# First products of sixteen full expert tiles computed during the state space model, and tiles over the usual number in conditional blocks

## Chip, core and metric

The kernel runs on one core of one Trainium2 chip. The metric is the device time of one execution in microseconds, as the median of several runs; a profiled execution gives the span and the trace that the text reads. The engines are called by their short names: PE is the matmul engine (PEld its weight loads), DVE the vector engine, ACT the activation engine, POOL the general one that also issues indirect transfers, SP the one that here only issues transfers. Everything is in 32-bit floats.

## What is computed

The input has 2 images of 256 channels and 48 × 48 points. A first layer (local attention of 7 × 7 plus a dynamic convolution) is followed by a second layer on the 4608 points as tokens of 256 values: a state space model and then a mixture of eight experts. Only the last is changed in substance:

```python
def _L1_ffn_ref(x, Wg, bg, W1, b1, W2, b2):
    xf = x.reshape(-1, D)
    gate_logits = xf @ Wg + bg
    top_w, top_i = jax.lax.top_k(gate_logits, TOP_K)          # TOP_K = 2
    top_w = jax.nn.softmax(top_w, axis=-1)
    w_dense = jnp.sum(jax.nn.one_hot(top_i, E, dtype=xf.dtype) * top_w[..., None], axis=1)
    out = jnp.zeros_like(xf)
    for e in range(E):                                        # E = 8
        h = jax.nn.gelu(xf @ W1[e] + b1[e], approximate=False)
        out = out + w_dense[:, e:e + 1] * (h @ W2[e] + b2[e])
    return out.reshape(B, L, D)

t = _to_tokens(x)
t = t + _L1_attn_ref(_ln_t(t), ...)                           # the state space model
t = t + _L1_ffn_ref(_ln_t(t), ...)                            # the experts
```

W1 is 256 × 1024 and W2 is 1024 × 256 for each expert. Each token goes to two experts, so there are 9216 rows of work, and how many fall on each expert is known only while the kernel runs.

## The kernel before

**Stages.** `run` issues three stages one after the other: `layer0` (the first layer), `mamba` (the state space model with the routing of the tokens), and `experts`. The memory of a stage (its pools) is given back at its end and used again by the next one.

**The state space model.** The 4608 tokens are 36 chunks of 128, in 12 blocks of three chunks. For a block, `norms`, `project_block` and `decays_of` make the normalized input, its projection, a convolution of four taps and the decays; for a chunk, `chunk` carries the state on and makes the output product (the matmul `out`, line 1419), after which the router's scores of the chunk are known. The chunks are routed in seven groups of 6, 6, 6, 6, 6, 4 and 2 (`GROUPS`). For a group, `gate` takes the top two experts of each token, counts how many rows each expert has so far (`g9`, kept in the tile `before`), and works out for every row its place in the table `xs` in HBM, which has a part of 4864 rows for each expert. The steps `put` (line 1628) scatter the rows of 265 values there (256 of the token, 8 expert weights, 1 token number) by indirect transfers of POOL, two for a chunk.

**What sets the order.** In this stage the order on PE, DVE, ACT and SP is written out ahead by a planner, the class `Flow`. Each step is added by `op` or `chain` with its engine, an estimated cost in ns, the steps that it needs, buffers that it takes and gives back (`room` says how many of each there are), and a due time: the number of its chunk times `PACE1`. The planner goes through a simulated time and starts, on each free engine, the step that is ready with the lowest rank; the rank is the due time less the length of the chain behind the step and less a figure of the step's kind from the table `LEAD1`. The result is the program order of the engines, and each engine executes its own queue strictly in this order. A transfer that SP issues has to wait for whatever produces its data, with everything behind it in SP's queue waiting too.

**The experts.** `experts` works on tiles of one expert's rows: a pair tile has 256 rows, a single tile 128. Since the counts are known only on the chip, the program has a fixed list: 36 pair tiles (`NPAIR`) and 8 single tiles (`NSINGLE`), one single after every four pairs. That is enough for any routing. `plan`, a chain of small DVE operations, makes from the counts two lists of where each tile's rows begin and which expert it has; what is over points to rows of zeros. `fill` writes 256 such rows behind the last row of each expert. For each tile, SP loads two numbers into registers (`value`) and issues the transfers with them (`fetch`: rows `ex`, weights `wt` of 2184 KB); `turn` transposes the rows on PE and copies them to `ext` by DVE, and takes the row weights; `up` is the first product, eight column blocks of two matmuls each, with bias and Gelu on ACT; `down` is the second product, 8 matmuls for each 128 rows into `po`, then bias and row weight on DVE, and an indirect transfer of POOL that adds the rows to `acc` in HBM. The loop is `up(i)`, `turn(i+1)`, `down(i)`, `fetch(i+3)`; there are three buffers of weights and four of rows. The very first tile always belongs to the first expert, and its weights (`first_weights`) are loaded during the state space model. At the end the sums in `acc` are loaded in twelve blocks by SP and ACT, transposed and written out.

Of the kernel before, what the change touches and what calls it, by code (L numbers as in the profile page):

```python
# [37 lines left out]
P = 128  # L38
# [38 lines left out]
NPAIR, NSINGLE = 2 * B * N // TR, E  # L77
NROWS = E * PART + TR
XW = C + E + 1
WCOL = NH * HID + NHC * C + NHC + C + E  # L80
# [143 lines left out]
class Kernel:  # L224
# [685 lines left out]
    def mamba(self, ctx):  # L910
# [8 lines left out]
                    mt=4, yi=1, y=4, sq=2, state=3, rd=2, u2=2)  # L919
# [12 lines left out]
        for g, n in enumerate(GROUPS):  # L932
            self.gate(g, first, n)
            first += n
        self.run_flow()

    PACE1 = 16387
    LEAD1 = {
        "al": -98773, "btt": 13567, "ct": -7065, "cum": 4429, "cv": 6696, "decayed": -3519, "dg":
        43691, "er": -366, "ex": -2395, "from": 164, "g10": 12483, "g5": -503, "g6": 8421, "g8":  # L940
        12831, "g9": 4638, "ge": -8611, "gm": 23689, "gmrs": 24439, "grs": -21221, "gsm": -10849,
        "gsw": 4862, "kap": 26098, "keep": -114, "lg": -10468, "mm": 2057, "mo": -5497, "mrr":
        10080, "mrs": -16433, "msw": -973, "mt": 8168, "n2": 1756, "n4": 12308, "nt": 100439,
        "number": 4867, "out": 3070, "pg": -32761, "place": 5798, "ps": -21172, "pst": 9783, "put":
        -196893, "py": 1458, "rd": -2334, "rg": -181, "row": 17176, "rs": -443, "rs1": 1733, "s0":
        443, "s4": 4537, "silu": -11890, "silub": 4711, "silux": -6634, "sm": -2191, "sq": -5514,
        "ss": -43075, "st": 864, "state": 16912, "stats": -2514, "su": -1714, "tap": 24701, "tb":
        2251, "tc": 62673, "tx": 5481, "u2": -20378, "xc": 12597, "xd": -222, "xo": -4221, "xt":
        45375, "xw": -105, "ya": 3557, "yb": 4919, "yi": -8286, "yz": 759, "z": -8801,
# [539 lines left out]
    def gate(self, g, first, n):  # L1489
# [135 lines left out]
        for i, c in enumerate(chunks):  # L1625
            for q in range(2):
                def put(i=i, q=q):
# [4 lines left out]
                    self.tc.declare_no_dep(ins.ins, group="rows", reason="every row of the table is written once")  # L1632
                    self.tc.add_to_no_dep_group("rows", ins.ins)
# [3 lines left out]

    def plan(self, pool):

# [8 lines left out]
        rows = new("rows", 2, E)  # L1648
        nc.vector.tensor_sub(rows[:, 0, :], self.taken, self.c["base"])
# [68 lines left out]
    def experts(self, ctx):  # L1718
# [12 lines left out]
        for i in range(NPAIR):  # L1731
            tiles.append((2, i))
            if i % every == every - 1 and i // every < NSINGLE:
                tiles.append((1, i // every))
# [238 lines left out]
```

## Time and profile before

| what | value |
|---|---|
| median of 3 runs | 1443.69 us (1443.32 to 1445.69) |
| span of the profiled execution | 1442.1 us (this run: 1443.9 us) |
| mean granted PE clock | 0.965 |
| PE busy in the span | 1312.6 us, 91% |
| DVE, ACT, POOL busy | 824.9, 757.6, 537.7 us |
| moved by DMA | 209.40 MB, mean 145 GB/s |
| last matmul of the state space model's output (line 1419) ends | 794.0 us |
| last scatter of rows lands | 822 us |
| first matmul of an expert tile, last one | 832.1 us, ends 1404.7 us |

Busy time is the time in which at least one instruction of an engine is under way. In the table of stretches that the prediction shows, a row is a stretch of the span in us, its length, then for PE, PEld, DVE, ACT and POOL the busy us and the number of instructions, then the granted clock, the busy share of the DMA engines, and GB/s. In the chain of waits a row is the start and length in us, the engine, what was written, the line and how many instructions were merged. A matmul of 32-bit floats leaves two records in this trace, so 16 matmuls appear as x32.

### The profile page before, as it was taken

How to read it: one execution, taken by the hardware profiler on the slowest of the kernel's cores; microseconds unless marked ns; L12 is line 12 of the kernel's file. 1: busy time of each engine (PE TensorE's matmuls, PEld its weight loads, DVE VectorE, ACT ScalarE, POOL GpSimd, SP SyncE). 2: the span in 40 equal slices, each digit the busy share in tenths (PEclk: the TensorE clock that was granted, in tenths of full speed). 3: DMA queues.
4: the chain of work that ended last, by engine and by line, in shares of the span. 5: the costliest groups of instructions: out<-in, count | busy, mean ns of one | idle time of the engine just before them, and what ended most of it. 6: DMA issues, size and time to landing. Idle time of an engine off the chain costs nothing.

```text
span 1442.1 us, 21771 instructions
## 1 busy us (share of the span) xinstructions
PE 1312.6 (91%) x7480; PEld 1028.6 (71%) x7480; DVE 824.9 (57%) x2165; ACT 757.6 (53%) x1840; POOL 537.7 (37%) x652
## 2 busy tenths in 40 slices
PE   5999999998999898988987099999999999999993
PEld 4566766666666665766665088888888888888883
DVE  5989999997799898999896321111111111111113
ACT  2688787897877767778765022222222222223220
POOL 5213030201666868776877511222212222222220
PEclk9999999998999999999999599999999999999996
DMA  8321412111432333323331276666667666676628
GB/s 289 99 84 44 146 36 94 45 54 67 129 91 81 117 91 101 104 78 118 100 112 52 98 280 216 224 215 196 222 209 225 201 225 205 202 227 215 225 27 266
DMA packets 102157, 209.40 MB, mean 145 GB/s; under 512 B 10251, under 2 KB 87260, under 8 KB 96092
## 3 DMA queue, kind: packets, MB, share of 16 engines
q1 hardware_dynamic: 81692, 181.06, 37.1%
q0 software_dynamic: 14976, 20.26, 7.4%
q10 hardware_dynamic: 5380, 6.69, 1.3%
q8 instruction: 60, 0.98, 0.3%
q14 instruction: 49, 0.40, 0.1%
HBM read 168.20 MB, written 44.71 MB: 148 GB/s over the span
## 4 chain that ended last, share of the span: by engine, by line
PE 53%; DVE 12%; POOL 5%; DMA 3%; issue 2%; ACT 2%; DVEq 0%; ACTq 0%; POOLq 0%; SPq 0%
PE bank L1787 19%; PE po L1801 19%; PE bank L908 3%; PE zbank L908 3%; POOL xs L1628 2%; PE bank L1419 2%; PE bank L894 2%; PE bank L1358 1%; PE bank L1401 1%; DVE xc L1105 1%; DMA out<-o 1%; DVE bc L1105 1%; DVE mt L1321 1%; DMA cz<-bc 1%; DVE yi L1378 1%
## 5 line engine op out<-in xcount | busy, mean ns | idle before, releaser
L1791 ACT ACTIVATE hid<-bank,wt 128x256 f32<-128x256 f32 (+1 forms) x352 | 160.1, 455 | 402.7 <-PE bank L1787 398.6
L1807 POOL DMA_INDIRECT acc<-ey,ex x80 | 124.6, 1557 | 462.6 <-DVE ey L1805 308.9
L1787 PE MATMUL bank<-ext,wt 128*128 128x256 f32 (+1 forms) x1408 | 286.2, 362 | 0.8 <-DVE ext L896 0.8
L1801 PE MATMUL po<-wt,hid 128*128 128x256 f32 x1280 | 283.7, 379 | 0.0
L1787 PEld LDWEIGHTS bank<-ext,wt 128*128 128x128 f32 x1408 | 249.8, 191 | 31.9 <-DVE ext L896 1.2
L1801 PEld LDWEIGHTS po<-wt,hid 128*128 128x128 f32 x1280 | 239.8, 190 | 30.8
L896 DVE COPY ext<-bank 128x512 f32<-128x512 f32 (+1 forms) x44 | 28.3, 643 | 231.4 <-PE bank L894 231.4
L1804 DVE TENSOR_TENSOR ey<-po,wt 128x256 f32<-128x256 f32 x80 | 34.0, 424 | 140.9 <-PE po L1801 140.8
L584 DVE SCALAR_TENSOR_TENSOR x<-hid,w2r,x 128x1128 f32<-128x1128 f32 (+3 forms) x72 | 99.9, 1393 | 0.4 <-ACT hid L578 0.2
L908 PE MATMUL bank<-xn,win 128*128 128x387 f32 x240 | 93.8, 514 | 0.4 <-DVE lg L1444 0.2
L673 POOL COPY kp<-kp 128x10 f32<-128x10 f32 (+1 forms) x60 | 23.6, 394 | 189.0 <-DVE kp L666 189.0
L1313 ACT ACTIVATE mt<-mt,cum 128x128 f32<-128x128 f32 x288 | 87.3, 396 | 0.0
L792 ACT ACTIVATE prob<-prob,top 128x308 f32<-128x308 f32 x144 | 78.2, 549 | 17.4 <-DVE top L781 17.0
L1105 DVE SCALAR_TENSOR_TENSOR xc<-bank,vec,xc 128x384 f32<-128x384 f32 x144 | 85.1, 605 | 1.5 <-ACT xc L1094 1.2
L1628 POOL DMA_INDIRECT xs<-u,rows x72 | 71.9, 999 | 22.5 <-issue 16.7
L908 PE MATMUL zbank<-xn,win 128*128 128x384 f32 x192 | 75.4, 517 | 4.5 <-ACT z L1215 4.5
L1419 PE MATMUL bank<-wout,y 128*128 128x264 f32 x288 | 72.1, 394 | 2.0 <-DVE ss L1434 1.6
L823 PE MATMUL bank<-pt,val 110*64 110x128 f32 (+1 forms) x864 | 69.5, 278 | 0.8 <-ACT pt L813 0.8
L798 ACT ACTIVATE prob<-prob,rden 128x308 f32<-128x308 f32 x144 | 67.7, 547 | 4.2 <-DVE rden L847 4.1
L823 PEld LDWEIGHTS bank<-pt,val 110*64 110x64 f32 (+1 forms) x864 | 58.7, 136 | 14.7 <-issue 10.0
L574 DVE SCALAR_TENSOR_TENSOR hid<-xp,vec,hid 128x1175 f32<-128x1175 f32 (+1 forms) x48 | 68.2, 1421 | 0.1
L781 DVE CUSTOM_DVE_ANT_0 prob<-banks,cst 128x308 f32<-128x308 f32 x144 | 61.7, 472 | 4.9 <-PE banks L771 4.7
(262 smaller groups left out, 2362.8 us busy)
## 6 DMA issues: line engine op xcount, KB each, us to landing
wt<-in_We SPq DMA_DIRECT2D x44, 2184.0 KB
mt<-decays SPq DMA_DIRECT2D x36, 512.0 KB
ex<-xs SPq DMA_DIRECT2D x36, 265.0 KB
rd<-decays SPq DMA_DIRECT2D x68, 128.0 KB
val<-vtab SPq DMA_DIRECT2D x72, 110.0 KB
vraster<-vout SPq DMA_DIRECT2D x18, 256.0 KB
acc<-x SPq DMA_DIRECT2D x36, 128.0 KB
vtab<-vraster SPq DMA_DIRECT2D x12, 304.0 KB
```

The source lines that it names most:

```text
L584: nc.vector.scalar_tensor_tensor(dst, src, w[:, k : k + 1], dst, ALU.mult, ALU.add)
L792: nc.scalar.activation(t, t, AF.Exp, bias=T["top", c][:, a : a + 1], scale=-1.0, accum_out=T["den", c][:, a : a + 1])
L823: nc.tensor.matmul(po[j * HD : (j + 1) * HD, :P], lhsT=T["val", c][:nk, i, a * HD : (a + 1) * HD], rhs=T["pt", key][:nk, j, i, :], start=i ...
L908: self.nc.tensor.matmul(ps, lhsT=lhs(k), rhs=rhs(k), start=k == 0, stop=k == NH - 1)
L1105: nc.vector.scalar_tensor_tensor(out(), T["bank", ("cv", at)][:, i : i + TB], wc[:, i : i + 1], out(), ALU.mult, ALU.add)
L1313: nc.scalar.activation(t, t, AF.Relu, bias=at_s, scale=-1.0)
L1419: nc.tensor.matmul(ps[:, : C + E], lhsT=T["y", c][:, m, :], rhs=self.l1["wout"][:, m, :], start=m == 0, stop=m == NZ - 1,)
L1628: ins = nc.gpsimd.indirect_dma_start(self.xs, bass.IndirectOffsetOnAxis(ap=of("rows")[:, i, q : q + 1], axis=0), T["u2", g][:, i, :], None,)
L1787: nc.tensor.matmul(ps[:, :rows], lhsT=w1[:, k, c * P : (c + 1) * P], rhs=xt[:, k, :], start=k == 0, stop=k == NH - 1,)
L1791: nc.scalar.activation(hid[:, c, :], ps[:, :rows], AF.Gelu, bias=b1[:, c : c + 1])
L1801: nc.tensor.matmul(po, lhsT=hid[:, c, j * P : (j + 1) * P], rhs=w2[:, c, :], start=c == 0, stop=c == NHC - 1)
L1807: put = nc.gpsimd.indirect_dma_start(self.acc, bass.IndirectOffsetOnAxis(ap=token, axis=0), y, None, compute_op=ALU.add)
```

## The change

Two constants name the early tiles: `EARLY = {1: 8, 3: 8}`, eight tiles after group 1 (12 chunks) and eight after group 3 (24 chunks), 16 in all (`NEARLY`).

1. *Early plan.* When a group of `EARLY` has been counted, `early_plan` works out with some 15 (group 1) or 21 (group 3) small DVE steps up to eight complete tiles of 256 rows: where the rows begin and which expert. `past` keeps how many complete tiles each expert has had.
2. *Early products.* For each of these tiles `early_product` adds steps to the planner: load the first weights and bias (1.05 MB, one buffer `w1`), load the rows (`fx`, after all scatters of the chunks counted), four transposes, a copy by DVE, then for four pairs of column blocks: two products of two matmuls each, the bias added by ACT or DVE in turn (no Gelu), and a store of 256 KB to a new array `hidden` in HBM.
3. *Room and pace.* The planner gets the new buffers (`w1`, `fx`, `ext` one each, `up` two) and other figures for `PACE1` (11733 for 16387) and `LEAD1`.
4. *The experts' list.* It now has the 16 early tiles, 20 pairs (`UPAIR`) and 4 singles (`USINGLE`): five early tiles first, then pairs, each followed by one early tile or a single while there are any. For an early tile `fetch` loads the last 9 columns of the rows, the second half of the weights (1.18 MB) and the hidden values (1.05 MB); `up` is only a Gelu in place (four ACT operations); `turn` has no transposes; `down` is unchanged. The columns of the weights in HBM are ordered anew, so that the bias of the first product stands beside its weights. `hid` has four buffers instead of two.
5. *Conditional blocks.* What is over the usual number stands behind the loop in nested `If` blocks: pairs from the 21st on in steps of 1, 1, 2, 4 and the rest, then singles from the fifth on one by one. Every engine loads the two counts into registers ahead of it.
6. *Start.* The early load of the first expert's weights is gone; the first three tiles of the list are fetched ahead of `plan` and of the fills.

The core of the diff:

```diff
+EARLY = {1: 8, 3: 8}
+NEARLY, NFIRST = sum(EARLY.values()), 5
+UPAIR, USINGLE = NPAIR - NEARLY, E // 2
...
-                    mt=4, yi=1, y=4, sq=2, state=3, rd=2, u2=2)
+                    mt=4, yi=1, y=4, sq=2, state=3, rd=2, u2=2, w1=1, fx=1, ext=1, up=2)
...
             self.gate(g, first, n)
             first += n
+            if g in EARLY:
+                self.early_plan(g, first)
+        self.early_products()
         self.run_flow()
-    PACE1 = 16387
+    PACE1 = 11733
...
+        op("fw", "queue", 3500, weights, ("ep", g), takes=[("w1", i)])
+        op("fx", "queue", 2800, rows, ("ep", g), *[("put", (c, q)) for c in range(first) for q in range(2)],
+           takes=[("fx", i)])
+        op("ft", "PE", 440, turn, ("fx", i), takes=[("bank", ("ft", i))], uses=[("fx", i)])
+        op("fc", "DVE", 660, lambda: nc.vector.tensor_copy(
+            self.large_tile("ext", i, [P, NH, TR]).rearrange("p k q -> p (k q)"), T["bank", ("ft", i)]
+        ), ("ft", i), takes=[("ext", i)], uses=[("bank", ("ft", i))])
...
+            def store(q=q, key=key):
+                nc.sync.dma_start(self.hidden[i, :, 2 * q : 2 * q + 2, :], T["up", key])
+            for h in range(2):
+                op(("fp", (i, q, h)), "PE", 890, partial(product, h), ("fw", i), ("fc", i),
+                   ("fp", (i, q, 0)) if h else None, takes=[] if h else [("bank", ("fp", key))], uses=[("ext", i)])
+            op(("fe", key), "DVE" if q % 2 else "ACT", 650 if q % 2 else 820, biased, ("fp", (i, q, 1)),
+               takes=[("up", key)], uses=[("bank", ("fp", key)), ("w1", i)])
+            op(("fs", key), "queue", 2200, store, ("fe", key), uses=[("up", key)])
...
+        early = [(0, i) for i in range(NEARLY)]
+        tiles, short = early[:NFIRST], early[NFIRST:] + [(1, i) for i in range(USINGLE)]
+        for i in range(UPAIR):
+            tiles += [(2, i), *short[i : i + 1]]
+        tiles += short[UPAIR:]
...
+                nc.sync.dma_start(x[:, :, C:], self.expert_rows(self.xs[bass.ds(row, TR), C:]))
+                nc.sync.dma_start(wt[:, W1COL:], ins["We"][bass.ds(part, P), W1COL:])
+                hidden[i] = hp.tile([P, NHC, TR], F32, tag="hid", name="hid", bufs=4)
+                last = nc.sync.dma_start(hidden[i], self.hidden[n])
...
+            if not rows:
+                for c in range(0, NHC, 2):
+                    part = hidden[i][:, c : c + 2, :]
+                    nc.scalar.activation(part, part, AF.Gelu)
+                return
...
-        fill(0)
-        fetch(0)
-        where = self.plan(plan)
+        for i in range(3):
+            fetch(i)
         turn(0)
-        for e in range(1, E):
+        where, many = self.plan(plan)
+        for e in range(E):
             fill(e)
-        fetch(1)
-        fetch(2)
...
+        run(0, usual)
+        all_engines = list(nc.engines)
+        many = [self.value(many[0:1, k : k + 1], all_engines, most) for k, most in enumerate((NPAIR, NSINGLE))]
+        for steps in rests:
+            with ExitStack() as nested:
+                for k, n, more in steps:
+                    nested.enter_context(self.tc.If(many[k] > n))
+                    first = len(tiles)
+                    tiles += more
+                    for i in range(first, min(first + 3, len(tiles))):
+                        fetch(i)
+                    turn(first)
+                    run(first, len(tiles))
...
-        self.first_weights = self.pool("ew0", 1).tile([P, WCOL], F32, name="wt")
-        nc.sync.dma_start(self.first_weights, self.ins["We"][0:P, :])
+        self.hidden = nc.dram_tensor("hidden", (NEARLY, P, NHC, TR), F32).ap()
```

## The prediction, made before the result was known

> **What bounds the kernel now.** I read three views in this order: the first two parts of the page, the table of engine time by stretch, and the chain of waits in order of time. The page first:
>
> ```profile
> span 1442.1 us, 21771 instructions
> PE 1312.6 (91%) x7480; PEld 1028.6 (71%) x7480; DVE 824.9 (57%) x2165; ACT 757.6 (53%) x1840; POOL 537.7 (37%) x652
> ...
> PE   5999999998999898988987099999999999999993
> DVE  5989999997799898999896321111111111111113
> ```
>
> TensorE is near full all along except in one hole, and the second digit row falls to 1 or 2 after slice 23: the experts are TensorE and its loads alone. The stretches around the hole (columns: stretch, length, then busy time and instruction count of PE, PEld, DVE, ACT, POOL, clock, DMA share, GB/s):
>
> ```profile
> 520.00:560.00 40.00, 37.46 (x230) 26.42 (x230) 38.55 (x123) 28.59 (x69) 28.73 (x33) 1.00 0.32 92
> ...
> 640.00:680.00 40.00, 35.46 (x215) 24.92 (x215) 38.36 (x100) 30.97 (x74) 30.90 (x37) 0.96 0.38 114
> ...
> 760.00:780.00 20.00, 14.76 (x84) 10.96 (x83) 12.65 (x36) 13.05 (x26) 15.56 (x17) 0.83 0.19 58
> 780.00:795.00 15.00, 10.99 (x74) 8.03 (x72) 10.82 (x43) 4.17 (x8) 14.11 (x19) 1.00 0.12 35
> 795.00:805.00 10.00, 1.61 (x8) 1.45 (x8) 5.31 (x40) 0.20 (x1) 7.54 (x8) 0.65 0.33 110
> 805.00:832.00 27.00, 1.09 (x4) 0.71 (x4) 7.04 (x37) 1.09 (x2) 10.77 (x12) 0.50 0.29 98
> ```
>
> From 520 to 795 PE is idle for only 29.9 of 275 us (the six 40 us rows of this stretch sum to 219.4 busy, the two shown add 25.8) and DVE, at 247.8, is as full. From 795 to 832 PE does nothing: the last group's routing runs on DVE and POOL. The chain of waits then gives the experts' price:
>
> ```profile
> 855.72 6.91 PE po L1801 x32
> 862.63 6.91 PE bank L1787 x32
> ...
> 876.88 6.91 PE bank L1787 x32
> 884.01 6.91 PE po L1801 x32
> 890.92 3.57 PE bank L1787 x32
> 894.93 3.46 PE po L1801 x16
> 898.38 6.91 PE bank L1787 x32
> ```
>
> A full tile takes 14.2 us on PE (6.91 first product, 6.91 second, about 0.4 transposes), a 128-row tile 898.38 − 890.92 = 7.46. All 36 + 8 tiles run back to back, 832 to 1405.
>
> [...] The trace has 6.91/32 = 216 ns per record[...]. [...] the first product of the first tile took 8.85 us (832.12 to 840.97), 1.9 over the others. [...] the trace reached 428 (842 to 846 us), so loads have room beyond the 200 to 225 of the experts. [...]
>
> **The change part by part.**
>
> *Removed from the experts.* Sixteen tiles lose first product and transposes: 16 × (6.91 + 0.4) = 117 us of PE. The unconditional 128-row tiles fall from eight to four: 4 × 7.46 = 30 us. Whether the conditional blocks run depends on the data. Routing the reference's own inputs by its formulas gives, after the 16 early tiles (8 complete of 8 slots after chunk 12, 12 of 8 after chunk 24), exactly 20 further pairs and 4 halves: the blocks are skipped. Together 147 us leave.
>
> *Added to the state space model.* Per early tile: 16 matmuls of 256 columns (6.91) and 4 transposes (0.43), and where eight groups alternate with other work each costs about 0.1 more (the 384-column groups start 1.40 apart, against 4 × 0.324 = 1.30): about 7.9 us with half of that and the wait after transposes. In the built instruction order, 13 of the 16 tiles lie on PE before the last output product (which ended at 794 in before), three (all of the second and third to last, most of the first) behind it. So 13 × 7.9 = 103 us come ahead of that point. I let the early work use 18 of the 29.9 idle us: one weight buffer means that a tile is not always ready, and the holes come when PE waits for DVE. Bounds: 0 and 29.9. That point moves to 794 + 103 − 18 = 879.
>
> DVE gets 16 × (0.69 + 2 × 0.68, by the 512-element rows from PSUM) = 33 us and some 40 planning operations of 0.2 = 8 us. Over a stretch that grows to 359 us, DVE's need of 248 + 41 = 289 stays below PE's: no cost. ACT's 64 reads of 256 columns at 0.47 = 30 us hide the same way, at 198 to 230 of 359.
>
> *SP's queue.* Each early tile puts a row load, a 1.05 MB weight load and four stores on SP: 96 more in-order transfers and 32 register loads (0.27 us). The row load waits for the scatters of its chunks; behind it stand the decay rows, the C copies and stores of later chunks, whose users are ACT, DVE and PE. At 428 GB/s one tile's 2.36 MB takes 5.5 us of the engines. I charge nothing for it, since DMA is busy a third of this stretch; the upper bound is the slow rival below. A gain from the planner's new figures (PACE1, LEAD1) is not excluded either; I take ±10 us for it.
>
> *The hole.* After the last output product: the tile at hand 7 us; its weight buffer is freed by the evictions (0.8), register load and issue 0.8, 1.05 MB landing 4.6 (estimate: 2.6 for the 265 KB row load issued at 826.97 and used at 829.6, plus 0.8 MB at 400 GB/s); a tile at the cold price, 8.8; again 6.2 and 8.8; evictions and last stores 3. Sum 40 us, against 28 before (794 to the landing of the last scatter at 822). So the hole absorbs three tiles and becomes 12 us longer.
>
> *Start of the experts.* The first fetch waits for everything of the stage before (its memory is reused): t0 = 879 + 40 = 919. Each early tile needs 2.23 MB (second weights 1.18, hidden values 1.05), 5.6 us at 400 GB/s. The first is ready at t0 + 10.5 (issues 1.8, latency 2, landing 5.6, first Gelu 0.6 and its wait), and takes 8.8; tiles two and three follow at 6.9 each, to t0 + 33. The fourth's load stands on SP behind the eight fills and waits for them, so it is ready at t0 + 37.5; fourth and fifth end at t0 + 51.5. The first full tile starts at t0 + 52 = 971. Before, fill, fetch and transpose cost 10 us and the early load of one weight set hid the rest.
>
> *The rest.* 20 × 14.2 + 11 × 6.91 + 4 × 7.46 = 390 us, at a DMA need of 4.68 MB + four scatters per 21.1 us, about 275 GB/s: below 428, so hidden. PE ends at 1361. From PE's last matmul to the end the old tail was 37.3 (1404.8 to 1442.1); it remains.
>
> *The conditional blocks.* On every engine two register loads wait for all work and every scatter, then two branches; queued behind are the final loads of acc on SP and ACT, and all of the output. Two register loads 0.6 us at least[...]. No row shows it; I take 6[...].
>
> Sum: 1361 + 37.3 + 6 = 1404.6 against a span of 1442.1, so −37.5. The runs stand 1.6 above the span (median 1443.7), so 1406.
>
> **The rivals.**
>
> 1. *Forecast (0.58):* holes half filled, SP harmless: 1406; its own range, with fill 5 to 28 us, branches 1 to 12, new planner figures ±10 and a few us of DMA lag, is 1386 to 1431.
> 2. *Better (0.14):* the new order also shortens the pure state space work, or the holes fill wholly: 1406 − 12 − 15 = 1379. For it: PE's digits of 8 in this stage; against it: DVE is at 38 of 40 us where PE idles.
> 3. *SP's in-order queue paces the state space model (0.16), slower:* each early tile's 5.5 us of transfers, or a load that waits with the decay rows behind it, delays the chunk chain instead of lying beside it. The gain of 37 us over 13 tiles is gone at 2.9 us a tile; at the full 5.5 the time is 1406 + 72 = 1478, and I name 1460 for it. For it: SP's queue already waits long (the waits view gives 83.5 us for the stores of acc on DVE). Against it: transfers take a third of the engines' time, and buffers (four decay rows) run ahead.
> 4. *PE only moved (0.12):* nothing fills and startup lags behind loads: 1406 + 18 + 12 = 1436; the four removed halves then pay for startup and branches alone. If routing on the chip gave one tile more than the usual number, a block of some 25 us (14.2 plus its own fetch) would give 1431 as well.
>
> **How the numbers follow.** A measurement of this kernel tells about 0.2%, 2.9 us, from no change. Cases 1 and 2 and nearly all of 4 are below 1440.8: 0.58 + 0.14 + 0.08 = 0.80 faster; within 0.2%: 0.04; slower 0.16, all from rival 3. The range from 1376 to 1450 takes in 1, 2, 4 and the lower part of 3.
>
> **What would show it.** Right: PE's last output product near 879; 3 early tiles in the hole behind it, apart by about 6 us; five second products ahead of the first transposes, the fourth late by some 4 us; full tiles still 14.2 us, early ones 6.9; end of matmuls near 1361 and a tail of 43. Wrong: PE busy below 90% from 520 on with waits for decay rows or C copies (rival 3); early tiles in the experts that start later than 6.9 us after each other while their weights land; matmuls of a conditional block; DVE rather than PE as the last releaser of the early products.

## The result, and the profile after

The changed kernel takes 1458.91 us (median of 4 runs, 1456.23 to 1460.9), against 1443.51 us for the kernel before beside it (4 runs, 1443.04 to 1445.69). The ratio is 1.0103, with an interval of 1.008 to 1.0126: slower by 1%, where the prediction had 2.6% faster. The profiled execution has a span of 1454.4 us, 12.3 longer than that of before (1442.1) and 50.1 longer than the sum of the prediction. (The terms of that sum, 1361 + 37.3 + 6, make 1404.3; the prediction wrote 1404.6.)

The first two parts of the page of the changed kernel:

```profile
span 1454.4 us, 21884 instructions
PE 1304.8 (90%) x7280; PEld 1012.6 (70%) x7280; DVE 843.1 (58%) x2225; ACT 739.9 (51%) x1807; POOL 531.8 (37%) x648
...
PE   5999999998899898899999897558999999999983
DVE  4989999997779899677687664322122122111113
```

PE lost only 7.8 us of busy time (1312.6 before) although 30 us of 128-row tiles are gone. The hole of PE (digits 5 and 5) is now two slices wide and begins at slice 26, about 910 us; before it was a zero in slice 23. And DVE's nines of the middle have turned into sixes to eights: the state space model has become slower for DVE too.

The table of stretches of the changed kernel (columns as in the prediction; the sum line is of seven stretches from 520 to 910):

```profile
520.00:560.00 40.00, 34.88 (x200) 24.12 (x198) 37.56 (x114) 30.22 (x71) 25.23 (x30) 0.96 0.33 89
...
640.00:680.00 40.00, 39.62 (x235) 30.71 (x234) 29.61 (x99) 26.51 (x64) 29.31 (x34) 1.00 0.58 183
...
760.00:800.00 40.00, 34.54 (x199) 25.91 (x198) 32.47 (x74) 15.06 (x30) 26.75 (x30) 0.96 0.33 99
...
880.00:910.00 30.00, 21.57 (x130) 18.02 (x128) 12.49 (x38) 6.19 (x13) 19.83 (x25) 0.89 0.57 176
910.00:960.00 50.00, 25.88 (x106) 21.37 (x104) 13.65 (x75) 6.25 (x17) 12.49 (x14) 0.85 0.45 149
...
sum 390.00, PE 352.44 PEld 266.55 DVE 279.97 ACT 226.06 POOL 220.66; mean PE 50.35 PEld 38.08 DVE 40.00 ACT 32.29 POOL 31.52
```

From 520 to the last output product at 910, PE is busy for 352.4 of 390 us, 90.4%. Before it was 245.1 of 275 (520 to 795), 89.1%. There are single rows that are full (39.62 of 40), but the idle time did not shrink: it went from 29.9 to 37.6 us. DVE is at 280 of 390, where it was at 247.8 of 275.

What PE waits for is no longer the same. These lines are from its waits from 520 to 910 (who waited, for whom; sum in us, times, longest). Line 1738 makes the transposes of an early tile; line 914 is shared by several products, and its waits for `w` and `ext` are those of early products; `up` is the step that adds the bias to an early product:

```profile
PE bank L914 <- DMA w<-in_We: 7.9, 3, 5.6
PE bank L1065 <- DVE lg L1455: 3.0, 1, 3.0
PE bank L1412 <- DVE gmv L1468: 2.8, 1, 2.8
PE bank L914 <- DVE ext L1744: 2.4, 1, 2.4
PE bank L1282 <- ACT up L1764: 2.3, 1, 2.3
...
PE bank L1738 <- DVE xc L1116: 2.2, 1, 2.2
```

Added up over PE's timeline, 21.1 of the 37.6 us stand ahead of a transpose or product of an early tile, 5.9 ahead of other steps that waited for a copy or bias step of an early tile, and 10.5 ahead of everything else, where before has all of its 29.9. So the early work took the place of some 19 us of the old waits and brought 27 us of its own. This says which step stood at the head of PE's queue, not whether the step behind it could have run.

What follows the last output product, from the timeline of PE in the changed kernel (start, length, line, operation, in brackets the idle time before it and what ended it):

```profile
928.04 8.90 PE L914 MATMUL bank<-ext,w 128*128 128x256 f32 x32 [8.15 <-DMA w<-in_We]
945.60 8.66 PE L914 MATMUL bank<-ext,w 128*128 128x256 f32 x32 [8.65 <-DMA w<-in_We]
970.10 23.86 PE L1971 MATMUL po<-wt,hid 128*128 128x256 f32 x96 [15.84 <-DMA wt<-in_We]
999.13 9.64 PE L1971 MATMUL po<-wt,hid 128*128 128x256 f32 x34 [5.17 <-ACT hid L1948]
...
1015.52 7.07 PE L1957 MATMUL bank<-ext,wt 128*128 128x256 f32 x32
```

Line 914 with `ext,w` is an early product, line 1971 a second product, line 1957 the first product of a full tile. The first row is the 15th early tile, which waits 8.15 us for its weights; the second is the 16th; then come three early tiles in the experts, the fourth after a wait, and at 1015.52 the first full tile. So 105 us lie between the last output product and the first full tile. Before it was 38.

Against before, the 12.3 us are made up so: the last output product ends 116.4 us later (794.0 to 910.4); from there to the end of the last matmul it takes 503.6 us instead of 610.7, which gives back 107.1; the tail after the last matmul is 40.4 instead of 37.4.

### The profile page after: what moved, and what is told of

The parts are those of the page before. It is cut to its first block, busy times and chain, and to the rows that moved or that the text cites. A ratio compares the mean times of both kernels' runs of the same rounds, so it can differ in the third digit from the quotient of the medians.

```text
span 1454.4 us, 21884 instructions
## 1 busy us (share of the span) xinstructions
PE 1304.8 (90%) x7280; PEld 1012.6 (70%) x7280; DVE 843.1 (58%) x2225; ACT 739.9 (51%) x1807; POOL 531.8 (37%) x648
## 4 chain that ended last, share of the span: by engine, by line
PE 35%; DMA 19%; DVE 12%; POOL 5%; issue 3%; ACT 2%; SPq 1%; DVEq 0%; ACTq 0%; POOLq 0%
PE bank L914 10%; PE po L1971 9%; DMA acc<-ey,ex 8%; PE bank L1957 6%; DMA wt<-in_We 3%; PE zbank L914 2%; PE bank L1430 2%; DVE xc L1116 2%; DMA w<-in_We 2%; POOL xs L1639 1%; PE bank L1412 1%; PE bank L1369 1%; DMA hid<-hidden 1%; POOL acc L1977 1%; DVE mt L1332 1%
## 5 line engine op out<-in xcount | busy, mean ns | idle before, releaser
L1971 PE MATMUL po<-wt,hid 128*128 128x256 f32 x1216 | 275.4, 386 | 22.5 <-DMA wt<-in_We 15.8
L1971 PEld LDWEIGHTS po<-wt,hid 128*128 128x128 f32 x1216 | 233.5, 194 | 56.0 <-issue 16.2
L1977 POOL DMA_INDIRECT acc<-ey,ex x76 | 118.5, 1559 | 365.8 <-DMA acc<-ey,ex 127.1
L1961 ACT ACTIVATE hid<-bank,wt 128x256 f32<-128x256 f32 (+1 forms) x192 | 84.7, 456 | 281.1 <-PE bank L1957 278.8
L1957 PE MATMUL bank<-ext,wt 128*128 128x256 f32 (+1 forms) x768 | 158.5, 365 | 3.0 <-ACT hid L1961 3.0
L1957 PEld LDWEIGHTS bank<-ext,wt 128*128 128x128 f32 x768 | 137.0, 192 | 21.2 <-ACT hid L1961 4.3
L914 PE MATMUL bank<-ext,w 128*128 128x256 f32 x512 | 120.9, 393 | 33.1 <-DMA w<-in_We 24.7
L914 PEld LDWEIGHTS bank<-ext,w 128*128 128x128 f32 x512 | 99.3, 197 | 51.6 <-issue 25.8
L1936 DVE TENSOR_TENSOR own<-ex,wt 128x16 f32<-128x16 f32 (+1 forms) x40 | 7.0, 174 | 220.9 <-DMA wt<-in_We 217.1
L1639 POOL DMA_INDIRECT xs<-u,rows x72 | 71.4, 992 | 28.3 <-issue 21.0
L914 PE MATMUL zbank<-xn,win 128*128 128x384 f32 x192 | 71.1, 494 | 0.6 <-ACT z L1226 0.6
L829 PEld LDWEIGHTS bank<-pt,val 110*64 110x64 f32 (+1 forms) x864 | 58.7, 136 | 14.7 <-issue 9.8
```

The source lines that it names most:

```text
L829: nc.tensor.matmul(po[j * HD : (j + 1) * HD, :P], lhsT=T["val", c][:nk, i, a * HD : (a + 1) * HD], rhs=T["pt", key][:nk, j, i, :], start=i ...
L914: self.nc.tensor.matmul(ps, lhsT=lhs(k), rhs=rhs(k), start=k == 0, stop=k == NH - 1)
L1639: ins = nc.gpsimd.indirect_dma_start(self.xs, bass.IndirectOffsetOnAxis(ap=of("rows")[:, i, q : q + 1], axis=0), T["u2", g][:, i, :], None,)
L1957: nc.tensor.matmul(ps[:, :rows], lhsT=w1[:, k, c * P : (c + 1) * P], rhs=xt[:, k, :], start=k == 0, stop=k == NH - 1,)
L1961: nc.scalar.activation(hid[:, c, :], ps[:, :rows], AF.Gelu, bias=b1[:, c : c + 1])
L1971: nc.tensor.matmul(po, lhsT=hid[:, c, j * P : (j + 1) * P], rhs=w2[:, c, :], start=c == 0, stop=c == NHC - 1)
```

## The experiments

All ratios are against the kernel before, run beside it on the same chip. There are four groups, each on one chip: e1 to e4, e5 to e8, e9 to e11, and e12 with e13. The kernel before takes 1443.5 us beside the change and 1445.3 to 1451.7 us in these groups, so small differences of times between groups mean little. In the table, T is the start of the last matmul of the output product in the profiled execution, and busy and idle are PE's from 520 us to T. "Ahead" is the number of early tiles that PE works on before T, from the timeline.

| run | ratio | interval | T | PE busy | idle | ahead |
|---|---|---|---|---|---|---|
| before (prediction's trace) | 1 | | 794 | 245.1 | 29.9 | 0 |
| the change | 1.0103 | 1.008 to 1.0126 | 910 | 352.4 | 37.6 | 13 |
| e1_singles | 0.9805 | 0.9777 to 0.9833 | 802 | 251.3 | 30.7 | 0 |
| e2_order | 1.0148 | 1.0117 to 1.0178 | 836 | 262.7 | 53.3 | 0 |
| e3_half | 0.9899 | 0.9869 to 0.993 | 895 | 316.4 | 58.6 | 13 |
| e4_actq | 1.0107 | 1.0073 to 1.0141 | 915 | 352.4 | 42.6 | 13 |
| e5_leads | 1.0089 | 1.006 to 1.0118 | 925 | 360.8 | 44.2 | 14 |
| e6_empty | 0.9584 | 0.9551 to 0.9616 | 867 | 274.1 | 72.9 | 0 |
| e7_three | 0.9774 | 0.9756 to 0.9793 | 795 | 246.7 | 28.3 | 0.6 |
| e8_two | 1.0018 | 1.0006 to 1.003 | 923 | 370.0 | 33.0 | 15 |
| e9_four | 0.9818 | 0.9786 to 0.985 | 802 | 254.9 | 28.1 | 0.6 |
| e10_eight | 0.9869 | 0.9834 to 0.9905 | 850 | 294.4 | 35.6 | 6 |
| e11_seq | 0.9942 | 0.9912 to 0.9972 | 920 | 361.4 | 38.6 | 14.1 |
| e12_emptyleads | 0.9683 | 0.9651 to 0.9715 | 887 | 284.5 | 82.5 | 0 |
| e13_cheap | 1.0423 | 1.0392 to 1.0454 | 991 | 391.9 | 79.1 | 16 |

(The before row ends at 795, as the prediction's rows do.)

### e1_singles: the conditional blocks alone

The kernel before, with four of its eight 128-row tiles in conditional blocks as in the change, and nothing else:

```diff
-            if i % every == every - 1 and i // every < NSINGLE:
+            if i % every == every - 1 and i // every < NSINGLE // 2:
                 tiles.append((1, i // every))
+        rests = [[(1, i, [(1, i)]) for i in range(NSINGLE // 2, NSINGLE)]]
```

> The kernel before with one part of the change alone: four of the eight single tiles go into conditional blocks, which this routing skips; no early tile. All theories expect four single tiles of 7.46 us less, 30 us, and some 4 us for the register loads and branches (the tail after the last matmul was 40.4 us after the change against 37.3): about 1417. If the blocks cost more than that, or if dropping the singles exposes loads of weights, it is above 1422.

0.9805, which is 28 us of 1451.7. The four tiles that are left out are worth 4 × 7.46 = 30 us of PE, so all but some 2 us arrive. This part of the change is a clear gain. It also means that the early tiles, as the change has them, cost more than the 1% that the whole shows: 2.98% between the two ratios, about 43 us. (T is 802 here with the state space model unchanged, and not 794; the kernel before itself takes 1451.7 us in this group, 8.2 more than the 1443.5 beside the change.)

### e2_order and e5_leads: the planner's new figures

e2_order is the kernel before with the new `PACE1` and `LEAD1` and no early work; e5_leads is the change with the old ones.

```diff
-    PACE1 = 16387
+    PACE1 = 11733
     LEAD1 = {
...
```

> The kernel before with only the planner's figures PACE1 and LEAD1 of the change, no early work. Theory 'PE full' (the early products lengthen the state space model by their own PE time and their own waits): no effect beyond 5 us, 1440 to 1448. Rival 'order' (the new figures make a worse order of the state space work itself): 1453 or more, and the last output product later than 800 us.

> The changed kernel with the planner's figures PACE1 and LEAD1 of before (steps of the early work have no figure and take 0). Theory 'order' (the new figures cost the state space model some 30 us, as they did without early work: last output product 836 against 802 in e1_singles on the same chip) expects 20 us or more less than the change, ratio to before 0.997 or lower. Theory 'mix' (the figures were right for the mix, and the early work itself costs what is lost) expects the same or slower, ratio 1.010 or higher.

Without early work the new figures cost 34 us (T 836 against 802 in e1_singles, whose state space model is that of before, on the same chip). Of these, 22.6 are idle time (53.3 against 30.7) and 11.4 busy time of PE. But with the early work the old figures give 1.0089 and the new ones 1.0103, with intervals that overlap. So with the early work there the choice of figures makes no difference that these runs can tell; it is not why the change is slower.

### e4_actq: the stores of the hidden values off SP's queue

```diff
-                nc.sync.dma_start(self.hidden[i, :, 2 * q : 2 * q + 2, :], T["up", key])
+                nc.scalar.dma_start(self.hidden[i, :, 2 * q : 2 * q + 2, :], T["up", key])
```

> The changed kernel with the 64 stores of hidden values issued by ACT instead of SP, so that SP's queue no longer waits for the evictions (137 us of waits on SP from 520 to 960 us are at these stores). 'SP queue' expects 15 us or more less, 1444 or below. 'PE full' expects no change within 5 us, 1454 to 1464.

1.0107: the same ratio as the change, within the intervals. Rival 3 of the prediction, whose sign came true, held that SP's queue paces the stage. With 64 of the 96 added transfers on another queue nothing moves, T included (915 on this chip, with 352.4 us of PE busy as in the change). In the change's trace these stores did wait on SP, 137 us in all from 520 to 960 for the ACT and DVE steps that make their data; with the stores gone from that queue T does not come earlier. The row and weight loads stayed on SP, so what they alone do was not tried.

### e3_half: half of the early matmuls

Of the two matmuls of each early column block only one is made, so the hidden values lack the second half of the sum. Everything else stays.

```diff
-                self.project(ps[:, h * TR : (h + 1) * TR], lambda k: w1[:, k, c * P : (c + 1) * P],
-                             lambda k: T["ext", i][:, k, :])
+                nc.tensor.matmul(ps[:, h * TR : (h + 1) * TR], lhsT=w1[:, 0, c * P : (c + 1) * P],
+                                 rhs=T["ext", i][:, 0, :], start=True, stop=True)
```

> The changed kernel with half of each early product left out: one of the two matmuls of each column block (the half sum over the second 128 input values is missing, so the output is not the reference's). Everything else stays: loads, transposes, evictions, stores, and the order. It takes 16 x 3.45 = 55 us of PE, 45 us of them ahead of the last output product. 'PE full' expects 40 to 55 us less, 1405 to 1420. Rival 'SP queue' (loads and stores of the early tiles delay the decay rows and C copies in SP's in-order queue) expects at most 15 us less, 1444 or more. 'Order' expects about 20 less.

PE's busy time before T falls by 36 us (352.4 to 316.4, e4_actq and e3_half on one chip), and T comes only 20 us earlier (915 to 895). The other 16 turn into idle time (42.6 to 58.6). So the price of an early tile does not follow its PE work alone: a microsecond of it taken away gives back 0.56. Most of the new idle time stands at the early work's other steps: PE waits 11.7 us at lines 1282 and 1287 for bias steps on ACT, against 1.2 in e4_actq, and 10.2 us for the rows of early tiles, against 3.0. The whole kernel gains 29 us on e4_actq (1436.0 against 1465.0), less than the 40 to 55 that 'PE full' asked for and more than the 'SP queue' theory allowed.

### e6_empty and e12_emptyleads: the order without the work

The steps of the early products stay in the planner with their costs, buffers and due times, but issue nothing; the experts read their "hidden values" from the weights' array. So nothing of the early products is computed. What is left is the order that the other steps have in the change (e6_empty), and the same planned with the old figures (e12_emptyleads).

```diff
         def op(name, engine, cost, make, *needs, **kw):
-            self.op(due, (name, i) if isinstance(name, str) else name, engine, cost, make, *needs, **kw)
+            self.op(due, (name, i) if isinstance(name, str) else name, engine, cost, lambda: None, *needs, **kw)
```

> The changed kernel with the planned order kept exactly, but all steps of the early products empty: no loads, transposes, products, evictions or stores (the hidden values are read from the weights' array instead, so the output is not the reference's; loads in the experts have the same size). It shows the state space work in the order of the change with nothing added. 'Order' expects the last output product near 836 us, as in e2_order, and so 75 to 80 us less than the change, ratio about 0.96. 'Early work costs its full time' expects it near 802 and a ratio of about 0.93. If the order laid out around the early work leaves gaps of its own, it stays above 850.

> As the change with all steps of the early products left empty (nothing of them is computed, and the experts' hidden values are read from the weights' array), but planned with the figures of before (PACE1, LEAD1). The empty run with the new figures ended its last output product at 867, some 65 us behind before, at 0.958. Theory figures: the new table alone is what opens these 65 us; with the old one the last output product ends near 802 to 815 and the ratio is 0.91 to 0.925. Theory spreading: the planner believes that the early steps take time and lays the other steps out around them, and queues that are executed strictly in order don't close these places whatever the table is; last output product still at 850 or later, ratio 0.945 to 0.965.

With none of the early work, the last output product still comes at 867, some 70 us after before's. (The small DVE steps of the early plan are still there; e7_three has those of one group, and its T is 795.) The table of stretches of e6_empty, and its sum from 520 to 867:

```profile
640.00:680.00 40.00, 33.16 (x189) 22.82 (x189) 27.93 (x67) 22.42 (x52) 30.85 (x34) 0.94 0.36 109
680.00:720.00 40.00, 32.84 (x172) 22.84 (x174) 27.25 (x71) 26.15 (x60) 19.22 (x25) 0.87 0.16 51
...
sum 347.00, PE 274.10 PEld 195.60 DVE 258.93 ACT 206.05 POOL 220.74; mean PE 39.16 PEld 27.94 DVE 36.99 ACT 29.44 POOL 31.53
```

Neither PE nor DVE nor any other engine is full, and yet the stage does not close up. The idle time of PE is 72.9 us. Its busy time is longer as well. At 520 the two kernels do not stand at the same matmul (e6_empty has 1550 records from there to T, before 1509), so I compare from 360 on, where both have some 2410 up to T: PE is busy for 419.6 us against 392.4, 27 us more for the same matmuls. The granted clock from 520 to T is 0.89, against 0.97 before (rows with gaps above: 0.94 and 0.87), and busy time multiplied by the granted clock of each stretch comes to about 382 us in one and 381 in the other. So the longer busy time goes with the lower granted clock. Most rows with more idle time have the lower clock (e6_empty has 0.85 with 32.11 of 40 us busy from 800 to 840, before has 1.00 with 38.48 from 680 to 720; but before also has 1.00 with 10.99 of 15 from 780 to 795). What lowers the clock no run isolates. In this pair the gaps came with a loss beyond their own length.

e12_emptyleads rules out that the new table does this: with the old one T is 887, with 82.5 us idle. What these two runs show is that an order written for certain work does not close up when the work is not there. They do not show that the change pays 70 us for its order, since there the work does stand in those places.

### e13_cheap: the work, planned as if it were nearly free

The opposite: all the work is done, but the planner is told an eighth of its cost, that of its loads and stores included, and has the old figures. It was meant to leave the other steps in nearly the order of before, with early tiles as lumps of up to 16 matmuls between them; all 16 lie ahead of the last output product.

```diff
-            self.op(due, (name, i) if isinstance(name, str) else name, engine, cost, make, *needs, **kw)
+            self.op(due, (name, i) if isinstance(name, str) else name, engine, cost // 8, make, *needs, **kw)
```

> The change with the figures of before and with the early steps planned at an eighth of their cost; all work is done. The order of the other steps then is nearly that of before, and an early tile mostly stands as one lump of 16 matmuls between them. The change with the figures of before gave 1.009 and an end of the last output product at 925. Theory spreading: with the order of before the places close, only the early work itself is paid; last output product at 875 to 895 and ratio 0.97 to 0.99. Theory full price: the early work costs its 8 to 9 us a tile in any order, because PE and DVE are both near full; last output product at 905 to 930, ratio 1.0 to 1.015. Above 1.02 would mean that lumps of 7 us hold up the chain of chunks more than finely mixed work does.

1.0423, beyond what both theories had: T at 991. The work comes for more, not for less. The stretches of e13_cheap show where, and the waits from 520 to 960 show how:

```profile
560.00:600.00 40.00, 28.93 (x164) 20.23 (x164) 26.68 (x71) 21.78 (x50) 27.21 (x31) 0.85 0.40 135
600.00:640.00 40.00, 32.70 (x139) 25.38 (x139) 15.11 (x40) 13.63 (x34) 5.46 (x7) 0.81 0.31 95
```

```profile
POOL y L1420 <- DVE y L1418: 47.0, 14, 19.9
DVE up L1759 <- PE bank L914: 44.4, 14, 14.7
...
ACT up L1762 <- PE bank L914: 35.1, 6, 10.6
DVE y L1418 <- PE bank L1410: 32.3, 7, 14.9
...
ACT up L1762 <- DMA hidden<-up: 27.4, 4, 14.3
...
PE bank L1736 <- DMA fx<-xs: 22.0, 4, 8.5
...
PE bank L914 <- DMA w<-in_We: 18.3, 4, 7.1
```

The last two lines are PE itself, waiting for the rows and the first weights of an early tile. Up to T they come to 22.0 and 26.4 of its 79.1 idle us. In e5_leads, which has the same table with the full costs, they are 8.9 and 7.7 of 44.2; so these two waits are 31.8 of the 34.9 us by which the idle time differs, on different chips. With loads that the planner takes for short, and one buffer each for rows and weights, the early step stands at the head of PE's queue before its data are there. So this run does not show what the work costs in the old order: the other steps are as near to that order in e5_leads as here (counted from the traces, 1.0% and 1.2% of the pairs of PE's other instructions have changed places against before).

The other engines wait in the same way. DVE stands up to 14.7 us, and ACT up to 14.3, at the head of their queues with such a step whose product or buffer is not there yet; the steps of the chain of chunks (`y`, `state`) are behind it, and POOL and PE wait for those in their turn. From 600 to 640 DVE, ACT and POOL are busy for only 15, 14 and 5 of 40 us. In the change itself the same waits are there, smaller. These lines are from its waits from 520 to 910:

```profile
DVE up L1761 <- PE bank L914: 19.9, 10, 5.8
...
ACT up L1764 <- PE bank L914: 18.6, 5, 11.7
...
DVE up L1761 <- DMA hidden<-up: 12.0, 5, 7.7
```

### e8_two and e11_seq: buffers

e8_two gives the early weights two buffers; the space comes from letting two small tiles of the early plan share one. e11_seq adds that the four column-block pairs of a tile are planned one behind the other, so that they hold one or two banks of PSUM at a time rather than four.

```diff
-                    mt=4, yi=1, y=4, sq=2, state=3, rd=2, u2=2, w1=1, fx=1, ext=1, up=2)
+                    mt=4, yi=1, y=4, sq=2, state=3, rd=2, u2=2, w1=2, fx=1, ext=1, up=2)
...
-                   ("fp", (i, q, 0)) if h else None, takes=[] if h else [("bank", ("fp", key))], uses=[("ext", i)])
+                   ("fp", (i, q, 0)) if h else ("fp", (i, q - 1, 1)) if q else None,
+                   takes=[] if h else [("bank", ("fp", key))], uses=[("ext", i)])
```

> The changed kernel with two buffers for the first weights (one small tile of the early plan shares another's memory to make room). The waits of PE for weights between early tiles (25 us in all, 17 of them behind the last output product) go. 'Weight buffer' expects 15 to 25 us less than the change, ratio 0.993 to 1.000; if the waits move elsewhere, 1.005 to 1.012. The order changes with the buffers, so a few us either way are open.

> As e8_two (the change with two buffers for the first weights), and the four column block pairs of an early product planned one after the other, so that they hold one or two of the six PSUM banks at a time and not four. 'Banks' (the state space steps wait for banks that the early products hold) expects the last output product 15 us or more ahead of e8_two's and a ratio of 0.992 or lower. 'PE full' expects 0.998 to 1.006, as e8_two.

The second buffer is worth 0.8% (1.0018 against 1.0103, the latter on another chip; 0.7% against e5_leads on its own chip, which has the old table). T hardly moves, 923 against 925 in e5_leads, but 15 tiles instead of 14 lie ahead of it, one is left for the hole, and the first fetch of the experts starts 28 us after T instead of 42 there and 49 in the change. So what the second buffer gains shows in the hole. e11_seq is between its two theories at 0.9942, with T at 920 and 19 us from T to the first fetch: again the hole. The waits of 8.15 and 8.65 us for weights, which the change has in the hole, are gone: the last early product waits there 7.07 us for its copy in e8_two and 0.26 us in e11_seq. Ahead of T less is gained: PE's 7.9 us of waits for `w` are gone in e8_two, and only 7.4 us of its idle time stand ahead of early steps instead of 21.1, but 10.1 instead of 5.9 go to their copies and bias steps and 15.4 instead of 10.5 to everything else. In all it is 33.0 and 38.6 us with more room and 37.6 without, for 15, 14.1 and 13 tiles, and the price of a tile stays (next section). More buffers for the rows or for `up` were not tried.

### e10_eight, e9_four, e7_three: fewer early tiles

All three have two weight buffers, the old figures, early tiles after group 3 only, and the unconditional list shortened to fit (with 4 singles and the conditional blocks). e10_eight spreads eight tiles as the change does; six lie ahead of T. e9_four and e7_three give all of theirs the due time `NCHUNK + 4`, behind everything else.

```diff
-EARLY = {1: 8, 3: 8}
-NEARLY, NFIRST = sum(EARLY.values()), 5
+EARLY = {3: 3}
+NEARLY, NFIRST = sum(EARLY.values()), 3
...
-                self.early_product(slot, g, j, ends[at], begin + (end - begin) * (j + 1) / n)
+                self.early_product(slot, g, j, ends[at], NCHUNK + 4)
```

> As e7_three with eight early tiles after group 3, due spread over the rest of the stage as in the change: in the built order six of them lie ahead of the last output product, two behind. Against e7_three the experts lose 5 x 7.3 = 36 us. 'Early work ahead of the last output product costs its full time and its share of the order' (113 us for 13 tiles in the change, 8.7 each) expects that product 45 to 52 us later and a ratio of 0.982 to 0.992. 'Holes fill' (half the PE time) expects it 20 to 25 us later and a ratio of 0.965 to 0.971.

> As e7_three with four early tiles, so that their loads of hidden values and second weights cover the wait of 6 us for the first full tile's weights there. The fourth product runs behind the last output product in the hole and may push the first fetch of the experts by 2 to 6 us; the experts lose 7.3 us. Theory 'only the hole is free': ratio 0.970 to 0.978. If the hole is already full with three, 0.978 to 0.983.

> The change cut down to what fits the hole: three early tiles (after group 3, all due at the end of the stage), two weight buffers, the planner's figures of before, 33 pairs and 4 singles, the rest in conditional blocks. 'Order' and 'PE full' both expect the state space model as in before (last output product at most 5 us later), the three products beside the last routing, and 3 x 7.3 = 22 us less in the experts than e1_singles less up to 10 us for the later start: ratio 0.97 to 0.98. If the early work costs more than its PE time through its loads and evictions, 0.985 or higher.

e10_eight and e9_four ran on one chip: T is 850.4 with 6 tiles ahead and 802.4 with 0.6 (20 of 128 records are before T). That is 48.0 / 5.4 = 8.9 us for a tile. The change has 116.4 / 13 = 8.95. e8_two against e7_three, on one chip: (923.3 − 795.2) / 14.4 = 8.9. In the same way e4_actq against e1_singles and e11_seq against e9_four give 8.7, and e5_leads against e7_three 9.7. Different mixes, two tables, one or two buffers: nearly the same price, the old table with one buffer the dearest. It does not hang on who waits for whom: of the 35.6 idle us in e10_eight only 7.6 belong to early work, and 28.0 are waits of the other steps as in e9_four. What a tile saves in the experts is 6.91 + 0.4 = 7.3 us. At 8.9 every early tile ahead of T loses about 1.6 us, 21 us for 13 tiles; the rest of the 43 us lies in the hole and behind it.

e7_three has the lowest ratio of the complete kernels, 0.9774, and is faster than both the kernel before and the change. Its early products lie beside the routing of the last groups; the timeline of PE around it:

```profile
799.59 5.42 PE L914 MATMUL bank<-ext,w 128*128 128x256 f32 x24 [1.01 <-DVE before L1598]
...
813.42 8.78 PE L914 MATMUL bank<-ext,w 128*128 128x256 f32 x32 [6.24 <-DVE ext L1742]
839.31 23.29 PE L1969 MATMUL po<-wt,hid 128*128 128x256 f32 x96 [17.11 <-ACT hid L1946]
...
869.40 9.79 PE L1955 MATMUL bank<-ext,wt 128*128 128x256 f32 x32 [6.36 <-DMA wt<-in_We]
```

Even so, its gain over e1_singles (0.9805) is 0.3%, with intervals that overlap; nearly all of it is the singles, and the early tiles alone show no gain that is clear of the noise. With a fourth tile the third and fourth products start at 819.6 and 829.8, the first weights of the experts are fetched 43 us after T instead of 34, and the ratio is 0.9818: no further gain, as expected if the hole is full with three, though the two intervals just touch.

## Why the prediction was wrong

The forecast was "1406, faster" with 0.80; the outcome is 1459, slower, to which it gave 0.16 by another cause. Step by step, with the sum of misses 31.4 + 8.6 + 4.6 + 8.5 − 3.0 = 50.1:

1. **The state space model, 879 predicted, 910.4 measured: +31.4. This is the step that failed.** It said "I let the early work use 18 of the 29.9 idle us". In sum none was used: the idle time grew to 37.6. The forecast left 11.9, so 25.7 us are here. The old waits did shrink, to 10.5 us by the count above, about as hoped; but 27.0 us of waits came with the early work, and the forecast had no term for them. The work itself was priced nearly right: 103 us predicted, 107.3 measured as the growth of PE's busy time. Per tile ahead of T the forecast came to (103 − 18) / 13 = 6.5 us, below the 7.3 that it saves; measured are 8.95, above it. This miss alone would still have left 6 us of gain (37.8 − 31.4); the 18.7 us of steps 5 to 8 make it the loss of 12.3. The bounds were wrong too: "0 and 29.9" let the early work at worst fill nothing, where added work can add idle time (e13_cheap: 189 us for 16 tiles, from 802, which is 11.8 each, a quarter of it waits for its loads).
2. **Why nothing is gained from the gaps.** Shown: it is not SP's stores (e4_actq), not the new table (e5_leads), and not PE's load alone (e3_half gets back 20 of 36 us); a second weight buffer and fewer banks at a time change the waits but not the price (e8_two, e11_seq). Shown also: an order is stiff. With work missing it stays long (e6_empty, e12_emptyleads). I read the idle tenth of PE in this stage as the cost of engines that wait for each other along the chain of chunks, each executing its queue in order; added steps join those queues and bring their own such waits, as the lines for `w` and `up` show. PE's busy share fits this: it is 89 to 92% from 520 to T in before and in every run whose early work is complete and planned at its cost (83% in e13_cheap), and the prediction's own 7.9 us of a tile divided by 0.891 is 8.9. But this is a reading: which queue's order sets the share was not isolated, and whether another order could use the gaps stays open.
3. **DVE charged at nothing: right in sum, misleading as a reason.** DVE's need was put at 289 of 359 us and is 280 of 390. No engine is full; no engine's sum of work is the bound.
4. **SP's queue charged at nothing: right for the stores**, as e4_actq shows; for the loads it was not tried. Rival 3 had the right sign, but the part of its mechanism that was tested did not hold.
5. **The hole, 40 predicted, 48.6 measured.** What the prediction calls the cold price, 8.8, was right: 8.90 and 8.66, behind 8.15 and 8.65 us of idle time and at a granted clock of 0.80 and 0.82 (before had 8.85, at 0.61 from 832 to 836.5). The tile at hand took 9.5 us instead of 7. The wait for a weight load was put at 6.2 us; the trace has 8.15 and 8.65. The last evictions and stores took 4.7 instead of 3.
6. **The start of the experts, t0 + 52 predicted, t0 + 56.6 measured.** The first early tile came at t0 + 11.1 (predicted 10.5). The 2 us of latency in that sum are near what the 24 KB stores of the decays show in before: the load that waits for one is issued 1.7 to 2.1 us after the store (413.82 to 415.51, 566.29 to 568.43). The wait before the fourth was 5.2 (predicted about 4), and the matmuls behind it were slow: 9.64 for 34 records, at a granted clock of 0.76 from 999 to 1008, where 32 take 6.91 in back-to-back work.
7. **The rest, 390 predicted, 398.5 measured.** 4.6 us of it are idle time of PE, most of it a wait of 3.04 for hidden values at 1045.06. The prices of 14.2 and 6.91 hold within some 2% (7.07 in the rows above). Why a record takes 216 ns (6.91 / 32), no run shows; the sums of the prediction used the measured 6.91.
8. **The conditional blocks, 6 predicted, 3.0 measured** as the growth of the tail, 37.4 to 40.4. The 6, and the 1 to 12 in the forecast's range, were estimates that no row of before supports. The last scatter is issued at 1415.3 and the loads of `acc` at 1423.1, 9.1 us after the last matmul; before it was 5.0. Singles in blocks are worth what was said: 28 of 30 us.

Rival 4, "nothing fills and startup lags behind loads", is nearest to what came. Its price of 1436 allowed 18 us for the fill and 12 for the start. The measured terms of the same places are 31.4 and 21.7 (8.6 + 4.6 + 8.5), less 3.0 for the tail: 1404.3 + 50.1 = 1454.4 of span. It too had no term for idle time that the early work adds, and it forecast a faster kernel.

## What to carry to other kernels

Idle time that is strewn over a stage in which several engines hand small steps to each other, in an order fixed ahead, need not be room for more work; here it was not. A safer first price for added work is its full length at the stage's old busy share (here 352.4 / 0.891 = 395 us against 390 measured, and 294.4 / 0.891 = 330 against 330 in e10_eight), compared with what it saves elsewhere, per tile. It fails where the added steps wait for their own loads (e13_cheap: 440 against 471). A hole in which the engine waits as a whole, such as the routing here, holds a few tiles, but count how many go into it before it gets longer. And measure the parts of a change apart: here the small one (0.9805) was hidden under the large one.

## What was not expected of the hardware

The price of an early tile came out near 8.9 us in different mixes, while its matmuls and transposes take 7.3; half of the matmuls (e3_half) still cost (895 − 802) / 13 = 7.2. And leaving work out made PE's remaining matmuls longer: from 360 us to T they take 419.6 us in e6_empty instead of 392.4, at a granted clock of 0.89 instead of 0.97 from 520 on. PE is idle there for 87.4 us instead of 41.6, so 46 us of added idle time came with 27 us of slower matmuls: 1.6 us in all for each microsecond of it. That holds for this pair of runs; what sets the granted clock was not isolated.
